# Four row tiles for a depthwise convolution: the matmul form of one stage of a two-layer kernel is replaced

## The chip, the cores and the metric

The kernel runs on one core of a Trainium2 chip, as one program. The metric is the device time of one execution in microseconds (us). The time before is the median of three runs, 3564.99 us, between 3564.83 and 3570.47.

## What is computed

Two layers run after each other on an input of 32 images, 96 channels, 56 rows and 56 columns, all in float32.

```python
# layer 0
h = conv_general_dilated(x, conv_w, (1, 1), padding=((3, 3), (3, 3)), feature_group_count=96) + conv_b
h = transpose(h, (0, 2, 3, 1))
h = (h - mean(h, -1)) * rsqrt(var(h, -1) + 1e-5) * ln_g + ln_b
h = gelu(einsum('bhwc,cf->bhwf', h, w1) + b1)
h = einsum('bhwf,fc->bhwc', h, w2) + b2
x = transpose(h, (0, 3, 1, 2)) * layer_scale + x
# layer 1
x = silu(conv_general_dilated(x, conv_w, padding 2, 5x5 taps, per channel) + conv_b)
# ... then a selective scan along the 3136 positions of every image
```

The change lies in the first convolution (7x7 taps, every channel by itself), in the layout of its output, and in the loads and stores of the MLP that follows. The second convolution and the scan have the same instructions before and after.

## The kernel before

The input comes as one array of channel, row and column, where a "row" is one of 2 x 56 (the images in two sets of 16, `j` being the set) and a row of 896 floats (`COLS`) holds 16 images of 56 columns beside each other. So the partitions hold image rows, and a vertical neighbour is another partition, a horizontal one another column.

A depthwise convolution becomes a matmul if the vertical taps are put into a matrix that multiplies rows by rows (a band matrix), one for each horizontal offset. The kernel before does this for two columns of the output at once. The input columns are separated into even and odd ones; the odd ones lie in partitions 0 to 55 of the tile `xq`, the even ones in partitions 64 to 119. The stationary matrix has 120 rows and 112 columns: 56 output rows for each of two neighbouring output columns. With 7 taps, four offsets `t` are enough, so each channel and set of images needs four matmuls with a moving operand of 448 columns (16 images x 28 column pairs), which add up in a bank of PSUM (L334). Copies of POOL (set 0), DVE (set 1) and ACT (both) bring the columns of `xt` apart into `xq` (L328, L329), so that the moving operand is contiguous within an image. A zero border of `xq` stands for the columns beyond the edge.

The band matrices are not built on the chip for each channel. A padded table `pad1` of the taps is written to memory once (`taps1_d`), and `taps_of` loads a channel's matrices by a DMA whose source addresses overlap (each row starts one step further on), into one of five tiles `wts`. In the matmul the weights of one `t` lie four floats apart (`wv`).

The loop runs over 112 jobs: the first 80 channels with both sets of images together, then the last 16 channels (`APART`) for set 0 and again for set 1, so that the statistics of set 0 are finished while set 1 is still computed. In each job ACT evicts the bank and adds the bias (L343), POOL issues two stores of the result to `conv1_d` (L347), and DVE and ACT keep the sums for the layer norm over channels: the difference to the first channel (L356), its sum (L357), its square on ACT (L358), the sum of squares (L359). `finish_norm` makes 1/standard deviation from them and writes it to `rstd_d`. Beside the loop, one entry of a list `beside` per job prepares weights of later stages. The order of instructions on an engine is made by the tile scheduler, except where `pin` keeps the program's order.

The MLP works on 28 groups of four rows. Each group has three tiles `h` of 32 channels x 4 rows, loaded from `conv1_d`; `rt`, the group's `rstd`, loaded to all channels; and three tiles of the input `x` for the residual. `normalise` multiplies h by rt on DVE (L412). `hidden` runs four row tiles of TensorE beside each other (32 rows each, one for each image row of the group, written to four banks, L422) and ACT applies gelu; `result` runs four column tiles (L441), and two DVE instructions add bias and residual and put even and odd column pairs into the output tile (L452). POOL's queue stores it to `block_d` (L464), which has four columns of a row apart from each other, as the second convolution reads them. The MLP's tiles `x`, having memory of their own, are loaded during the first convolution.

The second convolution (L535, L549, L558) uses four column tiles. The scan (L590 on) is a loop of DVE scans, products on POOL, activations and small matmuls.

Of the kernel before, what the change touches and what calls it, by code (L numbers as in the profile page):

```python
# [8 lines left out]
F32 = mybir.dt.float32  # L9
# [14 lines left out]
WP = 128  # L24
W2 = W // 2
MP = 64
P1 = (K1 + 1) // 2
# [3 lines left out]
RW = 32  # L31
QP = QW + 1
# [6 lines left out]
EPS = 1e-9  # L39
APART = 16  # L40
# [7 lines left out]
def convnext_then_scan_kernel(  # L48
# [30 lines left out]
    conv1_d = dram.tile([C, ROWS, COLS], F32, name="conv1_d")  # L79
# [3 lines left out]
    rstd_d = dram.tile([ROWS, COLS], F32, name="rstd_d")  # L83
    taps1_d = dram.tile([C, 3 * WP * P1], F32, name="taps1_d")
# [21 lines left out]

    KR = MP + H
    PQ = HALF

# [8 lines left out]

    front = ctx.enter_context(ExitStack())
    stats = front.enter_context(tc.tile_pool(name="stats", bufs=1))  # L120
    first = stats.tile([ROWS, B2, HALF], F32, name="first")
    acc1 = stats.tile([ROWS, B2, HALF], F32, name="acc1")
    acc2 = stats.tile([ROWS, B2, HALF], F32, name="acc2")
    sq = stats.tile([ROWS, B2, HALF], F32, name="sq")

    def finish_norm(j):

        a1, a2 = acc1[:, j], acc2[:, j]
        nc.vector.tensor_mul(sq[:, j], a1, a1)
        nc.vector.scalar_tensor_tensor(  # L130
            a2, in0=sq[:, j], scalar=-1.0 / C, in1=a2, op0=ALU.mult, op1=ALU.add
        )
        nc.vector.tensor_scalar(a2, a2, 1.0 / C, 0.0, ALU.mult, ALU.max)
        nc.scalar.activation(a2, a2, AF.Sqrt, bias=eps_t[:ROWS], scale=1.0)
        nc.vector.reciprocal(a1, a2)
        for s in range(2):
            nc.gpsimd.dma_start(
                rstd_d[j * H : (j + 1) * H, s * PQ : (s + 1) * PQ], a1[s * H : (s + 1) * H]
            )

    with tc.tile_pool(name="c1", bufs=3) as pool, tc.tile_pool(
        name="c1k", bufs=1
    ) as keep, tc.tile_pool(name="prep", bufs=1) as prep, tc.tile_pool(
        name="c1_ps", bufs=4, space=PSUM
    ) as psum:
        wts = [keep.tile([128, 2, H * P1], F32, name=f"wt1_{i}") for i in range(5)]
        xqs = [keep.tile([128, B2, BI, W2 + 3], F32, name=f"xq_{i}") for i in range(3)]
        jobs = [(c, (0, B2)) for c in range(C - APART)]
        jobs += [(c, (j, j + 1)) for j in range(B2) for c in range(C - APART, C)]


        kt1 = prep.tile([C, K1, K1], F32, name="kt1")
        nc.sync.dma_start(kt1, c1w.rearrange("c (i j) -> c i j", j=K1))
        xts: dict = {}

        def load_x(n):
            c, js = jobs[n]
            xts[n] = pool.tile([128, COLS], F32, name=f"xt1_{n}", tag="xt")
            for j in range(*js):
                nc.sync.dma_start(xts[n][MP * j : MP * j + H], x[c, j * H : (j + 1) * H])  # L160

# [13 lines left out]
        c1b_t = across(c1b, ROWS, C, "c1b_t", const)  # L175
        pad = prep.tile([C, 3, WP, P1], F32, name="pad1")
        nc.vector.memset(pad, 0.0)
        at = H - 1 - K1 // 2
        for i in range(3):
            for t in range(P1):  # L180
                j = 2 * t + 1 - i
                if j in range(K1):
                    nc.vector.tensor_copy(pad[:, i, at : at + K1, t], kt1[:, :, j])
        nc.sync.dma_start(taps1_d, pad.rearrange("c d p t -> c (d p t)"))
        for t in wts + xqs + [acc1, acc2]:
            nc.vector.memset(t, 0.0)
# [119 lines left out]
        def taps_of(n):  # L306

            c, wt = jobs[n][0], wts[n % len(wts)]
            for s in range(2):
                taps = bass.AP(  # L310
                    taps1_d.tensor, taps1_d.offset + (c * 3 + 1 - s) * WP * P1,
                    [[P1, H], [WP * P1, 2], [1, H * P1]],
                )
                nc.sync.dma_start(wt[MP * s : MP * s + H], taps)

        for n in range(4):
            taps_of(n)
        for n, (c, js) in enumerate(jobs):
            if n + 4 < len(jobs):
                taps_of(n + 4)  # L320
            if n + 2 < len(jobs):
                load_x(n + 2)

            xq, xt = xqs[n % len(xqs)], xts.pop(n)
            for j in range(*js):
                xv = xt[MP * j : MP * j + H].rearrange("p (i r s) -> p s i r", i=BI, s=2)
                copy = nc.vector.tensor_copy if j else nc.gpsimd.tensor_copy
                copy(xq[:H, j, :, 2 : W2 + 2], xv[:, 1])  # L328
                nc.scalar.copy(xq[MP:KR, j, :, 1 : W2 + 1], xv[:, 0])  # L329
            wv = wts[n % len(wts)].rearrange("p o m -> p (o m)").rearrange("p (q t) -> p t q", t=P1)  # L330
            ps = bank(f"ps1_{n}")[:ROWS, :, :PQ]
            for t in range(P1):
                for j in range(*js):
                    nc.tensor.matmul(  # L334
                        ps[:, j].rearrange("p (i r) -> p i r", i=BI),
                        lhsT=wv[:KR, t],
                        rhs=xq[:KR, j, :, t : t + W2],
                        start=(t == 0),
                        stop=(t == P1 - 1),
                    )  # L340
# [574 lines left out]
```

## Time and profile before

| | value |
|---|---|
| median of three runs | 3564.99 us |
| profiled execution | 3567.29 us |
| its span, first to last instruction | 3565.5 us |
| first convolution: first to last matmul of L334 | about 17.7 to 601 us |
| MLP | about 606 to 1425 us |
| second convolution | about 1425 to 1750 us |
| scan | the rest |
| PE busy over the span | 3047.3 us (85%) |
| DVE, ACT, POOL busy | 2664.8, 2351.5, 1969.4 us |
| mean granted clock of TensorE | 0.83 |

The profile is one execution on the chip. An engine's row gives its busy time; PEld is the weight load of TensorE, which runs beside matmuls. A group of instructions reads: line, engine, operation, tile written and tiles read, shapes, count, then busy time, mean nanoseconds of one instruction, and the idle time of the engine just before, with what ended it. In shapes like `32*128`, the first number is rows of the array, the second its columns. A float32 matmul leaves two records. The means of matmuls are longer than their pace, since they are pipelined: pace is busy time by count.

The input and the convolution's output are moved in these issues (the line names the tile written and the tensor read, the queue, the count and the size of one):

```
xt<-in_x_dram SPq DMA_DIRECT2D x192, 196.0 KB
x<-in_x_dram SPq DMA_DIRECT2D x336, 112.0 KB
h<-conv_d SPq DMA_DIRECT2D x336, 112.0 KB
conv_d<-ht POOLq DMA_DIRECT2D x158, 196.0 KB, 3.8
block_d<-o POOLq DMA_DIRECT2D x336, 120.0 KB, 3.1
```

### The profile page before, as it was taken

How to read it: one execution, taken by the hardware profiler on the slowest of the kernel's cores; microseconds unless marked ns; L12 is line 12 of the kernel's file. 1: busy time of each engine (PE TensorE's matmuls, PEld its weight loads, DVE VectorE, ACT ScalarE, POOL GpSimd, SP SyncE). 2: the span in 40 equal slices, each digit the busy share in tenths (PEclk: the TensorE clock that was granted, in tenths of full speed). 3: DMA queues.
4: the chain of work that ended last, by engine and by line, in shares of the span. 5: the costliest groups of instructions: out<-in, count | busy, mean ns of one | idle time of the engine just before them, and what ended most of it. 6: DMA issues, size and time to landing. Idle time of an engine off the chain costs nothing. (4 is left out here: it accounts for less than half of the span.)

```text
span 3565.5 us, 47085 instructions
## 1 busy us (share of the span) xinstructions
PE 3047.3 (85%) x17290; PEld 1291.7 (36%) x17290; DVE 2664.8 (75%) x1820; ACT 2351.5 (66%) x2168; POOL 1969.4 (55%) x1284
## 2 busy tenths in 40 slices
PE   8999999999999999799857777777777777777785
PEld 5777776333333333334322222222222222222221
DVE  6666667333333333799959999999999999999998
ACT  4555555334334333688778888888888887888885
POOL 2333343222222222000059999999899999999996
PEclk9999999999999999999956766666666666667666
DMA  6655556555555552899888787787778787887873
GB/s 185 194 178 167 173 168 197 159 159 162 162 161 164 164 159 67 244 280 290 273 257 278 264 281 261 268 279 256 264 263 270 267 272 250 290 259 260 287 255 120
DMA packets 316654, 793.97 MB, mean 223 GB/s; under 512 B 133560, under 2 KB 195024, under 8 KB 291880
## 3 DMA queue, kind: packets, MB, share of 16 engines
q1 hardware_dynamic: 269888, 671.99, 59.6%
q0 software_dynamic: 29632, 80.27, 7.0%
q10 hardware_dynamic: 16904, 38.70, 2.8%
q8 instruction: 137, 2.24, 0.3%
q14 instruction: 93, 0.76, 0.1%
HBM read 555.05 MB, written 235.74 MB: 222 GB/s over the span
## 5 line engine op out<-in xcount | busy, mean ns | idle before, releaser
L713 POOL TENSOR_TENSOR rep<-rep,bt 128x1568 f32<-128x1568 f32 x192 | 674.3, 3512 | 377.7 <-DMA rep<-du_d 377.7
L742 POOL TENSOR_TENSOR hs<-hs,ct 128x1568 f32<-128x1568 f32 x191 | 669.3, 3504 | 101.3 <-DVE hs L730 89.6
L723 DVE TENSOR_TENSOR_SCAN pv<-rep,pv 128x1568 f32<-128x1568 f32 x192 | 664.5, 3461 | 42.9 <-ACT rep L709 26.2
L432 ACT ACTIVATE g<-ph,b1p_t 128x896 f32<-128x896 f32 x336 | 320.0, 1003 | 489.7 <-PE ph L422 489.7
L452 DVE SCALAR_TENSOR_TENSOR o<-po,b2r_t,x 128x224 f32<-128x224 f32 x336 | 191.0, 611 | 545.5 <-PE po L441 534.7
L334 PE MATMUL ps<-xq,wt 120*112 120x448 f32 x1536 | 582.5, 540 | 17.7 <-DMA wt<-taps_d 17.7
L464 POOL DMA_DIRECT2D block_d<-o x336 | 183.1, 552 | 637.1 <-DVE o L452 603.9
L334 PEld LDWEIGHTS ps<-xq,wt 120*112 120x112 f32 x1536 | 429.3, 280 | 169.1 <-issue 20.2
L422 PE MATMUL ph<-h,w1r_t 32*128 32x448 f32 x4032 | 430.2, 555 | 6.9 <-DVE h L412 4.8
L641 PE MATMUL pz<-xs,wd_t 96*96 96x392 f32 x512 | 282.1, 718 | 164.6 <-ACT du L649 121.6
L441 PE MATMUL po<-g,w_t 128*32 128x448 f32 x4032 | 413.1, 543 | 0.0
L760 PE MATMUL py<-hs,sel_t 128*32 128x392 f32 x1536 | 323.1, 676 | 60.5 <-POOL hs L742 60.5
L688 PE MATMUL pk<-bn,pick_t 8*128 8x392 f32 x1024 | 291.7, 692 | 95.0 <-ACT y L769 83.1
L726 DVE SCALAR_TENSOR_TENSOR pv<-pv,rep 128x1568 f32<-128x1568 f32 x192 | 345.6, 1800 | 21.6 <-POOL rep L713 1.7
L730 DVE TENSOR_TENSOR_SCAN hs<-rep,carry_h,pv 128x1568 f32<-128x1568 f32 x96 | 334.1, 3480 | 10.0
L535 PE MATMUL ps<-xq,wt 128*32 128x448 f32 x3072 | 308.6, 549 | 37.5 <-DMA xq<-block_d 35.5
L558 DVE COPY st<-yt 28x896 f32<-28x896 f32 x288 | 318.0, 1104 | 27.8 <-ACT yt L549 17.5
L730 DVE TENSOR_TENSOR_SCAN hs<-rep,pv 128x1568 f32<-128x1568 f32 x96 | 328.4, 3421 | 9.6
L708 ACT ACTIVATE rep<-rep,lift_t 128x1568 f32<-128x1568 f32 x192 | 307.6, 1602 | 6.3
L709 ACT ACTIVATE rep<-rep,lift_t 128x1568 f32<-128x1568 f32 x192 | 307.6, 1602 | 6.3
L752 PE MATMUL py<-xs,dsm_t 96*96 96x392 f32 x512 | 300.7, 728 | 10.5 <-ACT bn L676 4.7
L707 ACT ACTIVATE rep<-rep,a_t 128x1568 f32<-128x1568 f32 x192 | 308.3, 1606 | 1.7 <-DMA rep<-du_d 1.3
(90 smaller groups left out, 3136.8 us busy)
## 6 DMA issues: line engine op xcount, KB each, us to landing
rep<-du_d SPq DMA_DIRECT2D x191, 1568.0 KB
du_d<-du SPq DMA_DIRECT2D x126, 588.0 KB
xq<-block_d SPq DMA_DIRECT2D x192, 225.0 KB
block_d<-o POOLq DMA_DIRECT2D x336, 120.0 KB, 3.1
xt<-in_x_dram SPq DMA_DIRECT2D x192, 196.0 KB
x<-in_x_dram SPq DMA_DIRECT2D x336, 112.0 KB
h<-conv_d SPq DMA_DIRECT2D x336, 112.0 KB
conv_d<-st SPq DMA_DIRECT2D x96, 392.0 KB
```

Of the source, the lines that this page charges most:

```text
L334: nc.tensor.matmul(ps[:, j].rearrange("p (i r) -> p i r", i=BI), lhsT=wv[:KR, t], rhs=xq[:KR, j, :, t : t + W2], start=(t == 0), stop=(t = ...
L422: pin(nc.tensor.matmul(phs[i // 2][:, i % 2, :HALF], lhsT=w1r_t[rows, d, f * 128 : (f + 1) * 128], rhs=hts[n, d][rows, s * HALF : (s + 1) ...
L432: nc.scalar.activation(gt, ph[:, :, :HALF], AF.Gelu, bias=b1p_t[:, f : f + 1], scale=1.0)
L441: pin(nc.tensor.matmul(po[CB * i : CB * i + CB, :HALF], lhsT=w2_t[:, f, CB * d : CB * d + CB], rhs=gts[n, s, f, i // 2][:, i % 2], start=( ...
L535: pin(nc.tensor.matmul(ps[RW * f : RW * f + RW, h, : B * QW].rearrange("p (b q) -> p b q", q=QW), lhsT=wv[:, f, t], rhs=xv[:, :, t : t + Q ...
L558: pin(copy(st[:, :, :, :, f], yt[RW * f : RW * f + QR].rearrange("p h (b q) -> p h b q", q=QW),))
L713: pin(nc.gpsimd.tensor_mul(ut, ut, bts[i // NG]))
L723: pin(nc.vector.tensor_tensor_scan(grown, da, zero, pv[:, last : last + 1] if q else 1.0 / EPS, ALU.mult, ALU.add))
L726: pin(nc.vector.scalar_tensor_tensor(run, in0=grown, scalar=1.0, in1=ut, op0=ALU.min, op1=ALU.mult))
L730: pin(nc.vector.tensor_tensor_scan(ht, da, run, carry_h[:, col : col + 1] if q else 0.0, ALU.mult, ALU.add))
L742: pin(nc.gpsimd.tensor_mul(ht, ht, cts[k]))
L760: pin(nc.tensor.matmul(py[g * DG : (g + 1) * DG, s, :BK], lhsT=sel_t, rhs=hss[k * NG + g][:, cols], start=False, stop=True, tile_position= ...
```

## The change

The first convolution is written anew. A job is now four pairs of a channel and a half `h` of the output rows: two channels with both halves (40 jobs), then for each half the last 16 channels by fours (8 jobs). Each pair takes 32 input rows (28 output rows and their neighbours inside the image) in 32 partitions, with all 32 images (1,792 columns). `load_x` brings them in as four DMAs, straight from the input, in the input's own column order; there is no `xq` and no copy into it.

`convolve` multiplies one column in four of the input (`g`, for every image and every fourth position, so the moving operand `xv[rows, g]` steps by four floats) by a matrix of 32 rows and 128 columns: 28 (of 32) output rows for each of four neighbouring output columns. Ten offsets `e` are needed for 7 taps and four columns. For six of the ten, an image's first or last column lies beyond the edge and is left out (`lo`, `hi`), so 13 of 14 positions are multiplied and written. The four pairs of the job sit in four row tiles (`tile_position=(RW * k, 0)`) and write four banks.

All ten matrices of a pair come from one tile `mat` of 13 blocks of 32 columns, seven with taps and three of zeros at each end; the matrix of `e` is the 128 columns from block `e` on. `turn` fills the seven blocks by an ACT copy from the loaded taps, which are smaller than before.

ACT evicts a job by two instructions of 896 columns or four of 448; the store is one DMA on ACT's own queue. The sums are kept for both channels of a job apart and added in `finish_norm`. The output in `conv1_d` and `rstd_d` is by half, column of four, row.

In the MLP a group is four rows of one half and two of the four columns. The loads of h and rt for the first two groups, and the first normalising, are called within the convolution's loop. The tiles `x` hold all four columns, are loaded for every second group, and come from a pool opened after the convolution's pools are closed. The result is added by one DVE instruction instead of two, and a row of four columns is stored as one piece of 7,680 bytes for each channel.

```diff
-    conv1_d = dram.tile([C, ROWS, COLS], F32, name="conv1_d")
+    conv1_d = dram.tile([C, 2, QC, RW, HALF], F32, name="conv1_d")
...
-    taps1_d = dram.tile([C, 3 * WP * P1], F32, name="taps1_d")
+    taps1_d = dram.tile([C, TP * K1], F32, name="taps1_d")
...
-        jobs = [(c, (0, B2)) for c in range(C - APART)]
-        jobs += [(c, (j, j + 1)) for j in range(B2) for c in range(C - APART, C)]
...
+        jobs = [[(c, 0), (c, 1), (c + 1, 0), (c + 1, 1)] for c in range(0, C - APART, 2)]
+        whole = len(jobs)
+        jobs += [
+            [(c + k, h) for k in range(JT)] for h in range(2) for c in range(C - APART, C, JT)
+        ]
...
+            xts[n] = pool.tile([128, 2 * COLS], F32, name=f"xt1_{n}", tag="xt")
+            for k, (c, h) in enumerate(jobs[n]):
+                nc.sync.dma_start(
+                    two(xts[n][RW * k : RW * k + RW]),
+                    x[c].rearrange("(j m) q -> m j q", m=H)[h * (H - RW) : h * (H - RW) + RW],
+                )
...
-            for j in range(*js):
-                xv = xt[MP * j : MP * j + H].rearrange("p (i r s) -> p s i r", i=BI, s=2)
-                copy = nc.vector.tensor_copy if j else nc.gpsimd.tensor_copy
-                copy(xq[:H, j, :, 2 : W2 + 2], xv[:, 1])
-                nc.scalar.copy(xq[MP:KR, j, :, 1 : W2 + 1], xv[:, 0])
-            wv = wts[n % len(wts)].rearrange("p o m -> p (o m)").rearrange("p (q t) -> p t q", t=P1)
-            ps = bank(f"ps1_{n}")[:ROWS, :, :PQ]
-            for t in range(P1):
-                for j in range(*js):
...
+            nc.scalar.copy(
+                mats[n % len(mats)][:, QC - 1 : QC - 1 + K1],
+                wts.pop(n).rearrange("p (o j) -> p j o", j=K1),
+            )
...
+            wv = mats[n % len(mats)].rearrange("p j o -> p (j o)")
+            xv = xts.pop(n).rearrange("p (b q f) -> p f b q", q=QW, f=QC)
+            pss = [bank(f"ps1_{n}_{a}") for a in range(JT // 2)]
+
+            order = sorted(range(EJ), key=lambda e: e != K1 // 2)
+            for e in order:
+
+                far, g = divmod(e - K1 // 2, QC)
+                lo, hi = max(0, -far), QW - max(0, far)
+                for k in range(JT):
+                    rows = slice(RW * k, RW * k + RW)
                     nc.tensor.matmul(
-                        ps[:, j].rearrange("p (i r) -> p i r", i=BI),
-                        lhsT=wv[:KR, t],
-                        rhs=xq[:KR, j, :, t : t + W2],
-                        start=(t == 0),
-                        stop=(t == P1 - 1),
+                        pss[k // 2][:, k % 2, :HALF].rearrange("p (b q) -> p b q", q=QW)[:, :, lo:hi],
+                        lhsT=wv[rows, RW * e : RW * e + QC * RW],
+                        rhs=xv[rows, g, :, lo + far : hi + far],
+                        start=(e == order[0]),
+                        stop=(e == order[-1]),
+                        tile_position=(RW * k, 0),
                     )
...
-            for s in range(2):
-                nc.gpsimd.dma_start(
-                    conv1_d[c, js[0] * H : js[1] * H, s * PQ : (s + 1) * PQ].rearrange(
-                        "(j m) q -> m j q", m=H
-                    ),
-                    ht[s * H : (s + 1) * H, half],
...
+            step = 2 if n < whole else 1
+            for k in range(0, JT, step):
+                c = job[k][0]
+                nc.scalar.activation(
+                    hs[:, k : k + step],
+                    pss[k // 2][:, k % 2 : k % 2 + step, :HALF],
...
+            nc.scalar.dma_start(to, hs)
...
+            def squares():
+                nc.scalar.activation(dt, dt, AF.Square)
+                for ks, _, a2 in parts:
+                    nc.vector.tensor_add(a2, a2, flat(dt[:, ks]))
...
+            pss = convolve(n)
+            if n == whole + len(jobs[whole:]) // 2:
+                finish_norm(0)
+            hs = evict(n, pss)
...
+            squares = add_sums(n, hs)
+            if n + 1 < len(jobs):
+                squares()
+            if n >= 2 and beside:
                 beside.pop(0)()
-            if n == C + 1:
-                finish_norm(0)
...
+            if n == len(jobs) - 3:
+                load_rows(0)
+                load_rows(1)
+            if n == len(jobs) - 2:
+                for d in range(blocks):
+                    normalise(0, d)
...
-            for e in range(2):
-                pin(nc.vector.scalar_tensor_tensor(
-                    ot[:, 2 * e + s, :, e : e + QW],
-                    in0=po[:, :HALF].rearrange("p (i a e) -> p e i a", i=BI, e=2)[:, e],
...
+            pin(nc.vector.scalar_tensor_tensor(
+                ot[:, f].rearrange("p (b r) -> p b r", r=QP)[:, :, at : at + QW],
+                in0=po[:, :HALF].rearrange("p (b q) -> p b q", q=QW),
+                scalar=b2r_t[:, d : d + 1],
+                in1=xts[n // 2, d].rearrange("p (b q f) -> p f b q", q=QW, f=QC)[:, f],
```

## The prediction, made before the changed kernel was run

> **What bounds the kernel now.** I read four views in this order. First the page: its slices of the span, and the groups of the line that is replaced.
>
> ```profile
> span 3565.5 us, 47085 instructions
> PE   8999999999999999799857777777777777777785
> ...
> L334 PE MATMUL ps<-xq,wt 120*112 120x448 f32 x1536 | 582.5, 540 | 17.7 <-DMA wt<-taps_d 17.7
> ...
> L334 PEld LDWEIGHTS ps<-xq,wt 120*112 120x112 f32 x1536 | 429.3, 280 | 169.1 <-issue 20.2
> L422 PE MATMUL ph<-h,w1r_t 32*128 32x448 f32 x4032 | 430.2, 555 | 6.9 <-DVE h L412 4.8
> ```
>
> Second the busy times by stage, with stretches cut at the first and last matmul of L334 (columns: length, then PE, PEld, DVE, ACT, POOL busy, clock, DMA share, GB/s).
>
> ```profile
> 17.70:601.00 583.30, 583.29 (x1546) 430.55 (x1546) 367.07 (x470) 307.57 (x413) 192.71 (x317) 1.00 0.61 183
> 601.00:612.00 11.00, 5.49 (x30) 2.47 (x28) 10.15 (x13) 3.67 (x6) 5.84 (x9) 0.84 0.75 232
> 612.00:1425.00 813.00, 811.61 (x8000) 302.79 (x8004) 269.67 (x413) 319.94 (x336) 178.41 (x327) 1.00 0.50 149
> ```
>
> The reader is to see that PE works without a gap for 583.3 us of convolution and for 811.6 of 813.0 us of MLP, at full clock, while DVE is at 63% and DMA at 61% in the first. TensorE bounds both, so what the first convolution costs TensorE is what it costs the kernel. The second convolution and the scan, from about 1425 us on, have the same instructions on both sides and keep their time.
>
> Third the timeline of one channel in the middle of the first convolution. L343 evicts at 300.09 and again at 306.12: 6.03 us a channel, which is 16 passes of 377 ns (a float32 matmul leaves two records; I call each a pass).
>
> ```profile
> 300.09 1.01 ACT L343 ACTIVATE ht<-ps,c1b_t 112x896 f32<-112x896 f32 x1 [0.16 <-PE ps L334]
> ...
> 302.25 1.09 DVE L357 TENSOR_TENSOR acc<-acc,dt 112x896 f32<-112x896 f32 x1
> 303.44 0.95 ACT L358 ACTIVATE dt<-dt 112x896 f32<-112x896 f32 x1 [1.72 <-DVE acc L357]
> 304.42 1.09 DVE L359 TENSOR_TENSOR acc<-acc,dt 112x896 f32<-112x896 f32 x1 [1.08 <-ACT dt L358]
> ...
> 306.12 1.01 ACT L343 ACTIVATE ht<-ps,c1b_t 112x896 f32<-112x896 f32 x1 [0.15 <-PE ps L334]
> ```
>
> Last the groups by shape, for what an access costs that steps over elements: the weight loads,
>
> ```profile
> L535 PEld LDWEIGHTS ps<-xq,wt 128*32 128x32 f32 x3072 | 133.2, 141 | 213.0 <-issue 194.6 <-ACT st L558 12.1 <-DMA xq<-block_d 4.1
> L441 PEld LDWEIGHTS po<-g,w_t 128*32 128x32 f32 x4032 | 114.1, 109 | 274.2 <-issue 223.4 <-DVE h L412 50.8
> ...
> L250 PEld LDWEIGHTS ps_b<-lnb_t,w_t 96*128 96x128 f32 x6 | 0.8, 190 | 0.3 <-issue 0.2
> L247 PEld LDWEIGHTS ps_w<-w1g,cen 96*96 96x96 f32 x2 | 0.3, 162 | 0.3 <-issue 0.2
> ```
>
> and, in the second convolution, a copy of ACT that writes one float in four:
>
> ```profile
> L558 ACT COPY st<-yt 28x896 f32<-28x896 f32 x96 | 195.8, 2040 | 53.9 <-DMA conv_d<-st 52.7
> ```
>
> These rows carry the forecast. With contiguous columns 96 take 162 ns and 128 take 190: 0.875 ns a column over a fixed 78. L334's weights lie four floats (16 bytes) apart: (280 - 78)/112 = 1.80 ns a column. L535's lie eight floats apart: 32 columns cost 32 ns more than L441's contiguous 32, so 1.88. TensorE reads float32 weights at half speed once each lies 16 bytes or more from the last. ACT shows the same: from the squares (448 elements 576 ns, 896 elements 950) it has 202 ns fixed and 0.835 an element, but writing every fourth float in L558 takes (2040 - 202)/896 = 2.05.
>
> **What the Trainium skill says.** "SBUF — State Buffer", section "Door 1: The DMA port swizzle", describes 16-byte lines that give full bandwidth only when hit at least twice; the loads above agree. The same note puts the free step at four float32 elements; L334's 1.80 against 0.875 contradicts that, and the measurement decides. "TensorE: Matmul & The Clock Gate", section "LDWEIGHTS", prices a load by its columns alone, P/1.2 ns; the slope of 0.875 agrees for contiguous weights, not for stepped ones. The same page, Part 3, gives 3.07 times for four row tiles side by side. Here L422, in the very form that the change uses, needs 430.2/4032 = 107 ns a pass against 379 for L334: 3.6 times. No page says how fast a stepped moving operand streams, and no matmul of this trace has one.
>
> **The change part by part.**
>
> *Matmuls of the first convolution.* Removed: 768 matmuls, two passes of 448 columns, 688,128 column steps in 582.5 us, 0.8465 ns a step. Added: 48 jobs of ten input columns; for each, four row tiles beside each other, so the set of four costs the steps of one. Four of the ten sets are 448 columns wide, six are 416: 2 x (4 x 448 + 6 x 416) = 8,576 steps a job, 411,648 in all. Contiguous, that would be 348.5 us. But the moving operand is read from x as it lies, every fourth float, where before xq was contiguous. Contiguous float32 weights go in at 0.875 ns an element and contiguous moving data at 0.8465, the same pace, so I expect the same halving. Bounds: 0.8465 ns a step if the moving path hides it (348.5 us), 2.05, as in ACT's stepped copy (844 us). I take twice 0.8465, 1.693: 697 us, 14.5 a job, **114.5 more than before**. The six narrower sets also write PSUM in runs of 13, which no row of the trace shows; I give that nothing, and the range's upper side holds it. The weights are now contiguous and load under the matmuls.
>
> *Beside it, per job of 14.5 us.* DVE: three operations on 1,792 elements. From 624 ns for 448 and 1,092 for 896 (1.045 an element, 156 fixed) each is 2.03, so 6.1 us. ACT: two evictions of 1.01, the square 202 + 1792 x 0.835 = 1.70, and the new turn of the taps, 128x224, 0.4 contiguous and 0.7 at half speed, so 4.4 us. DVE's order is strict: difference, first sum, then the second sum, which waits for ACT's square; the next difference is queued behind it. ACT in turn has the next eviction behind that square. The ring costs 2.03 + 2.03 + 0.1 + 1.70 + 0.05 + two evictions 2.02 = 7.95 us: free under 14.5, dear if the matmuls are fast. Gone are the xq copies of ACT, DVE and POOL, none on the path.
>
> *DMA.* A job moves 917 KB in, 917 KB out, 115 KB of taps: 1.95 MB per 14.5 us, 134 GB/s, below the 183 of now. Stores move from POOL's queue to ACT's; issuing is short beside ACT's 10 us of slack.
>
> *Start.* PE waits 17.7 us for taps. The table is smaller (183 KB for 590), but eight loads of x of 229 KB stand before it on SP's queue where four of 196 did, and a turn follows: -2 to +3, taken as +1.
>
> *Passage to the MLP.* Today PE idles about 6.9 us there, 4.8 of it for DVE's normalised h. The first half's norm is now finished at job 44, with three jobs behind it, and the first h are normalised in the loop: -5 (0 to -7). The loads of x for the MLP can no longer come early, as their memory is the convolution's: 2.75 MB, some 11 us at the 250 GB/s that the scan's slices of the page reach, while PE has 12 us of hidden layer before the first result asks for them and two result banks after that. Nothing, up to +8 if that cover fails.
>
> *MLP and its end.* The same passes in the same order, so 812 us. DVE's two additions of 611 ns become one of 448 elements, 0.6 to 1.1 us, with DVE idle two thirds of the time: nothing. Stores of block_d become whole rows, but the last are twice as large, 240 KB, with the second convolution waiting for them: +3 (0 to +6).
>
> *Sum* on the profiled execution: 3567.3 + 114.5 + 1 - 5 + 3 = 3680.8; the median of the runs shown is 2.3 lower. With 1.70 instead of 1.693 ns (the loads suggested 1.80 to 1.88) another 3 us: **3682 us**.
>
> **The rivals.**
>
> *Full-speed moving operand (ends faster).* Mechanism: the moving path streams steps of 16 bytes at 0.8465 ns. For it: nothing in the trace shows a stepped moving operand, and it is a read port of its own. Against: weights, and ACT's writes, all halve. Matmuls then take 7.26 us a job, the ring of DVE and ACT 7.95 takes over: 40 x 7.95 + 8 x 8.5 (four short evictions, sums in halves) = 386, plus some 8 us of backlog before the MLP: 3567.3 - 582.5 + 386 + 8 - 2.3 = 3376 us. It decides below 582.5/411,648 = 1.415 ns a step; above that the kernel is slower.
>
> *Partly slowed*, 1.0 to 1.6 ns a step: 412 to 659 us, so 3395 to 3642; half of it on either side.
>
> *Tiles one after another.* The change then doesn't do what it says: 4 x 348.5 = 1394 us, 4377. Against it L422's 107 ns in the same form, with the same four banks.
>
> **How the numbers follow.** Half speed or slower 0.83, full speed 0.11, partly 0.04, serial 0.02. The range runs from 3645 (half speed less the edges, and the upper end of partly) to 3800 (1.98 ns a step); left out are full speed, most of partly, serial, and 0.05 of the forecast's own case. Only cases of one sign hold most of the chance. A measurement here tells about 0.2% (7 us) from no change. Faster: 0.11 + 0.02 = 0.13; within: 0.01; slower: 0.86.
>
> **What would show it.** Right: sets of four matmuls of L368 every 0.70 to 0.76 us, PE without gaps, jobs 14.5 us apart, DVE and ACT each below half busy, DMA share below 0.5. Wrong: sets every 0.36 us and idle PE before L368 released by ACT's evictions, which is the first rival; or matmuls of one set following each other, which is the last. The MLP should stay at about 812 us of PE. A gap of over 5 us after the last L368, released by the DMA of x, would break the passage.

## The result: 4.4% slower, and the profile after

| | before | after |
|---|---|---|
| median (range, runs) | 3565.36 us (3564.83 to 3570.47, 4) | 3723.52 us (3721.39 to 3724.39, 4) |
| ratio, 95% interval | | 1.0439 [1.0421, 1.0457] |
| span of the profiled execution | 3565.5 us | 3721.6 us |
| first convolution, first matmul to last | 17.7 to 601 | 24.1 to 759.2 |

The forecast was 3682 us in a range of 3645 to 3800; the time is 41.5 us above the forecast and inside the range. These are lines of the page of the changed kernel: the span, TensorE's row of slices, and the groups of the new matmul and its weight loads.

```profile
span 3721.6 us, 49078 instructions
...
PE   7999999999999999989976777787777787777775
...
L368 PE MATMUL ps<-xt,mat 32*128 32x416 f32 (+1 forms) x3840 | 733.8, 936 | 24.1 <-ACT mat L351 24.1
...
L368 PEld LDWEIGHTS ps<-xt,mat 32*128 32x128 f32 x3840 | 445.8, 204 | 308.2 <-issue 256.8
```

TensorE was busy for 582.5 us in the first convolution before; now it is busy for 733.8, and its only idle time is the 24.1 us at the start. The busy times by stage (length, PE, PEld, DVE, ACT, POOL, clock, DMA share, GB/s) say what holds it:

```profile
24.10:759.20 735.10, 735.09 (x3850) 446.94 (x3850) 303.51 (x178) 202.03 (x206) 0.73 (x1) 1.00 0.45 133
759.20:784.00 24.80, 16.89 (x102) 7.45 (x104) 15.42 (x13) 14.03 (x15) 8.79 (x6) 0.72 0.87 206
784.00:1580.00 796.00, 796.00 (x7864) 296.42 (x7860) 245.41 (x243) 312.21 (x328) 75.39 (x156) 1.00 0.50 150
```

In the convolution PE has no gap, at full clock; DVE is at 41%, ACT at 27%, DMA at 45%. Nothing but the matmul itself can be the limit. The timeline of one job shows its pace. The weight loads stand for the matmuls here, four loads to a set: one pass of 448 or 416 columns, done by four row tiles at once. The first two load lines belong to sets of 416 columns, the last two to sets of 448.

```profile
300.69 1.01 ACT L388 ACTIVATE hs<-ps,c1b_t 128x896 f32<-128x896 f32 x1 [7.21 <-PE ps L368]
...
303.97 0.52 PEld L368 LDWEIGHTS ps<-xt,mat 32*128 32x128 f32 x4 [0.23 <-issue]
304.71 0.52 PEld L368 LDWEIGHTS ps<-xt,mat 32*128 32x128 f32 x4 [0.23 <-issue]
...
308.48 0.61 PEld L368 LDWEIGHTS ps<-xt,mat 32*128 32x128 f32 x4 [0.18 <-issue]
309.27 0.60 PEld L368 LDWEIGHTS ps<-xt,mat 32*128 32x128 f32 x4 [0.18 <-issue]
...
315.94 1.01 ACT L388 ACTIVATE hs<-ps,c1b_t 128x896 f32<-128x896 f32 x1 [7.21 <-PE ps L368]
```

From load to load over several sets, a set of 416 columns takes 0.745 us, one of 448 takes 0.787, and a job has 12 of the first and 8 of the second: 15.24 us. The evictions at 300.69 and 315.94 are one job apart, 15.25 us. The tiles do run side by side: one after another, a set would take four passes of 377 ns. The eviction waits 7.21 us for the matmuls, so ACT follows and doesn't lead.

Where the 156 us of span come from (each from the views shown here, before against after):

| part | us |
|---|---|
| matmuls of the first convolution, 733.8 against 582.5 | +151.3 |
| first matmul at 24.11, not 17.71 | +6.4 |
| last matmul of the convolution to last matmul of the MLP, 830.9 against 827.3 | +3.6 |
| PE's gap ahead of the second convolution, 11.32 against 13.62 | -2.3 |
| the rest, second convolution and scan | -2.9 |

The +6.4 is in the timeline of the start:

```profile
1.20 12.83 SPq L190 DMA_DIRECT2D xt<-in_x_dram  x8
...
15.25 0.33 SPq L212 DMA_DIRECT2D taps_d<-pad  x1
...
19.73 5.42 SPq L343 DMA_DIRECT2D wt<-taps_d  x12
```

The table of taps is in its tile `pad` by 4.5 us, but its store is issued only at 15.25, behind eight issues of x that took SP's queue 12.83 us; then the round trip through memory and ACT's turn follow. At the passage to the MLP the three idle times of PE are:

```profile
760.48 4.97 PE L504 MATMUL ph<-h,w1r_t 32*128 32x448 f32 x28 [1.26 <-ACT hs L388]
768.84 4.04 PE L504 MATMUL ph<-h,w1r_t 32*128 32x448 f32 x24 [3.39 <-ACT g L514]
776.14 7.76 PE L504 MATMUL ph<-h,w1r_t 32*128 32x448 f32 x44 [3.26 <-ACT g L514]
```

Before, there were two:

```profile
606.30 4.97 PE L422 MATMUL ph<-h,w1r_t 32*128 32x448 f32 x28 [4.78 <-DVE h L412]
613.02 2.25 PE L422 MATMUL ph<-h,w1r_t 32*128 32x448 f32 x12 [1.75 <-ACT g L432]
```

The wait for DVE's first h is gone, as forecast, but in place of one wait of 1.75 us for ACT's gelu there are two, of 3.39 and 3.26. ACT takes the square root of the second half's norm between two gelus there: it loads its tables three times (1.28 us each; two of the three are shown) and waits 2.1 us for DVE's variance (L133).

```profile
769.70 1.28 ACT L134 ACT_TABLE_LOAD   x1
773.10 0.67 ACT L134 ACTIVATE acc<-acc,eps_t 128x448 f32<-128x448 f32 x1 [2.11 <-DVE acc L133]
773.78 1.28 ACT L514 ACT_TABLE_LOAD   x1
```

The page's group of the hidden layer sums it up (before: 430.2 us busy, 6.9 idle):

```profile
L504 PE MATMUL ph<-h,w1r_t 32*128 32x448 f32 x4032 | 432.9, 558 | 7.9 <-ACT g L514 6.6
```

So 1.0 of the 3.6 us is idle time. The rest is busy time, and it falls in the stretch of these waits (759.20 to 784.00 above, with a mean granted clock of 0.72): after it the mean of a hidden-layer matmul is 551 ns on both sides.

### The profile page after: what moved, and what is told of

Its sections match the earlier page's. It is cut to its first block, busy times and chain, and to the rows that moved or that the text cites. A ratio compares the mean times of both kernels' runs of the same rounds, so it can differ in the third digit from the quotient of the medians.

```text
span 3721.6 us, 49078 instructions
## 1 busy us (share of the span) xinstructions
PE 3195.8 (86%) x19594; PEld 1305.0 (35%) x19594; DVE 2581.1 (69%) x1370; ACT 2249.4 (60%) x1963; POOL 1676.2 (45%) x796
## 5 line engine op out<-in xcount | busy, mean ns | idle before, releaser
L368 PE MATMUL ps<-xt,mat 32*128 32x416 f32 (+1 forms) x3840 | 733.8, 936 | 24.1 <-ACT mat L351 24.1
L536 DVE SCALAR_TENSOR_TENSOR o<-po,b2r_t,x 128x448 f32<-128x448 f32 x168 | 170.5, 1015 | 564.8 <-PE po L523 552.3
L368 PEld LDWEIGHTS ps<-xt,mat 32*128 32x128 f32 x3840 | 445.8, 204 | 308.2 <-issue 256.8
L547 POOL DMA_DIRECT2D block_d<-o x168 | 81.2, 490 | 734.9 <-DVE o L536 678.8
```

What stands on the lines that cost most here:

```text
L368: nc.tensor.matmul(pss[k // 2][:, k % 2, :HALF].rearrange("p (b q) -> p b q", q=QW)[:, :, lo:hi], lhsT=wv[rows, RW * e : RW * e + QC * RW] ...
```

## The experiments

The theory, from the prediction: the step of four floats in the moving operand is the whole loss, and with contiguous data the ring of DVE and ACT becomes the bound. Rivals: the narrower sets, a fixed cost for each set, or the four tiles hindering each other. Each edit is against the changed kernel unless another is named. Ratios are to the kernel before on the same chip, with the 95% interval; a single run has none.

**The step taken out, and halved, and made three.** The same matmuls read the tile with another view, and so multiply other columns.

```diff
-            xv = xts.pop(n).rearrange("p (b q f) -> p f b q", q=QW, f=QC)
+            xv = xts.pop(n).rearrange("p (f b q) -> p f b q", q=QW, f=QC)
```

For a step of two floats, and of three (which reads the first three quarters of the tile), the view and its index are:

```diff
+            xv = xts.pop(n).rearrange("p (t b q f) -> p t f b q", t=2, q=QW, f=2)
...
+                        rhs=xv[rows, g // 2, g % 2, :, lo + far : hi + far],
```

```diff
+            xv = xts.pop(n)[:, : 3 * HALF].rearrange("p (b q f) -> p f b q", q=QW, f=3)
...
+                        rhs=xv[rows, g % 3, :, lo + far : hi + far],
```

> The only edit is the view of the moving operand in the changed kernel's matmul: 448 (or 13 of each 14) neighbouring floats instead of every fourth, so the columns multiplied are other ones than the convolution's; sizes, weights, tiles, PSUM writes and all other work stay. Theory (a step of 16 bytes halves the stream of the moving operand, and nothing else is slow): L368 falls from 733.8 us to about 348 us of work, a set of four from 0.75-0.79 us to about 0.36; then the ring of DVE and ACT (difference, sum, square, second sum, evictions) sets a job at about 8.0 us, so the stage takes some 386 us and the kernel about 3723 - 734 + 386 + 8 = 3383 us, under 3400. Rival (the tile form itself is slow: runs of 13 written to PSUM, four banks, 128 weight columns loaded for each set): the pace stays at 0.75 us a set and the time within 1% of 3723. Rival (partly the step, partly the form): between 3450 and 3650.

> The moving operand steps by two floats (8 bytes) instead of four; again other columns than the convolution's, all else as in the changed kernel. Theory A (full pace as long as each 16-byte line is hit twice): as with contiguous columns, about 0.36 us a set and about 3383 us. Theory B (every step beyond one element costs): a set at 0.5 us or more, L368 over 480 us, the kernel over 3460.

> The moving operand steps by three floats (12 bytes), so that of four elements three open a new line; other columns than the convolution's. Theory A1 (each new 16-byte line costs two cycles[...], a second hit in it is free):[...] a set of 448 at about 0.56 to 0.6 us, L368 some 520 to 550 us, the kernel about 3510 to 3540. Theory A2 (a threshold at a step of 16 bytes, full pace below): about 0.36 us a set and 3383 us. Theory A3 (half pace as soon as a line is not hit twice by neighbours): 0.75 us and 3723.

Measured: 3391.32 us for the contiguous view (ratio 0.9507 [0.9491, 0.9523]), 3396.26 for two floats and 3549.43 for three (a single run each). The contiguous view alone takes 332 us off the changed kernel and makes it faster than the one before. The sets, from the timelines of a job as above (for one float from the kernel with the pinned order below, where no set waits), beside the number of 16-byte lines that a set's read goes through. A run of an image is 14 positions in the wide sets and 13 in the narrow, and lines are counted from the view, each run of neighbouring reads in one line once:

| step | set of 448, us | lines | set of 416, us | lines |
|---|---|---|---|---|
| 1 float | 0.374 | 112 | 0.351 | 112 |
| 2 floats | 0.394 | 224 | 0.395 | 224 |
| 3 floats | 0.59 | 336 | 0.567 | 320 |
| 4 floats (the change) | 0.787 | 448 | 0.745 | 416 |

The lines behind the table. For one float, two loads before sets of 448:

```profile
308.02 0.20 PEld L368 LDWEIGHTS ps<-xt,mat 32*128 32x128 f32 x4 [0.17 <-issue]
308.40 0.20 PEld L368 LDWEIGHTS ps<-xt,mat 32*128 32x128 f32 x4 [0.17 <-issue]
```

For two floats, sets of 448 and then of 416:

```profile
308.07 0.21 PEld L368 LDWEIGHTS ps<-xt,mat 32*128 32x128 f32 x4 [0.18 <-issue]
308.46 0.21 PEld L368 LDWEIGHTS ps<-xt,mat 32*128 32x128 f32 x4 [0.18 <-issue]
...
310.43 0.22 PEld L368 LDWEIGHTS ps<-xt,mat 32*128 32x128 f32 x4 [0.17 <-issue]
310.83 0.22 PEld L368 LDWEIGHTS ps<-xt,mat 32*128 32x128 f32 x4 [0.17 <-issue]
```

For three floats, the sets of 416 and then of 448:

```profile
308.20 0.23 PEld L368 LDWEIGHTS ps<-xt,mat 32*128 32x128 f32 x4 [0.33 <-issue]
308.77 0.23 PEld L368 LDWEIGHTS ps<-xt,mat 32*128 32x128 f32 x4 [0.33 <-issue]
...
311.12 0.21 PEld L368 LDWEIGHTS ps<-xt,mat 32*128 32x128 f32 x4 [0.38 <-issue]
311.71 0.21 PEld L368 LDWEIGHTS ps<-xt,mat 32*128 32x128 f32 x4 [0.38 <-issue]
```

The widest step gives 0.787/448 = 1.757 ns a line. With that price the other stepped sets come out at 224 x 1.757 = 0.394 (measured 0.394 and 0.395), 336 x 1.757 = 0.590 (0.59) and 320 x 1.757 = 0.562 (0.567); 112 lines would be 0.197, and there the floor of 0.835 ns a column stands (448 x 0.835 = 0.374). So in these runs a pass pays the larger of two sums: 0.835 ns for each column, or 1.757 ns for each new line. That it is lines and not bytes is seen at two floats: 13 positions touch seven lines as 14 do, and the narrow set is no shorter than the wide one. Only the narrow set of the change itself is clearly off, 0.745 for 416 x 1.757 = 0.731.

Two of the rivals go with the first row. The four tiles don't hinder each other: side by side they take 0.374 us, where one pass of as many columns took 0.377 alone in the kernel before (120 rows, contiguous). And the narrower sets, which write PSUM in runs of 13, take 0.351 for 416 x 0.835 = 0.347.

The Trainium skill's "SBUF — State Buffer", section "Door 1: The DMA port swizzle", speaks of 16-byte lines that need two hits for full bandwidth. The runs nearly agree: at two floats, so two hits, a column costs 0.88 ns for 0.835. Its "4 fp32" as the free stride is contradicted, as by the weight loads before: at four floats a column costs 1.757 ns.

The contiguous view also shows the next bound. The timeline of one job of it:

```profile
308.30 2.02 DVE L433 TENSOR_TENSOR acc<-acc,dt 128x1792 f32<-128x1792 f32 x1 [1.76 <-ACT dt L431]
...
310.25 2.02 DVE L416 TENSOR_TENSOR dt<-hs,first 128x1792 f32<-128x1792 f32 x1
312.30 2.02 DVE L428 TENSOR_TENSOR acc<-acc,dt 128x1792 f32<-128x1792 f32 x1
314.36 1.70 ACT L431 ACTIVATE dt<-dt 128x1792 f32<-128x1792 f32 x1 [3.80 <-DVE acc L428]
315.96 1.89 ACT L388 ACTIVATE hs<-ps,c1b_t 128x896 f32<-128x896 f32 x2
316.08 2.02 DVE L433 TENSOR_TENSOR acc<-acc,dt 128x1792 f32<-128x1792 f32 x1 [1.76 <-ACT dt L431]
```

DVE's second sum (L433) waits for the square, ACT's evictions come after the square, and DVE's next difference after both: 7.78 us from one L433 to the next, the ring that the prediction put at 7.95. The matmuls need 8 x 0.374 + 12 x 0.351 = 7.2 and wait. The step of two floats lies just beside it: 20 sets of 0.395 make 7.9 us a job, so its time is near the contiguous view's.

**More and shorter sets** (eight of the ten sets cut in two halves of the images).

```diff
-                for k in range(JT):
+                cuts = [(0, B)] if e in (order[0], order[-1]) else [(0, BI), (BI, B)]
+                for (s, z), k in [(cut, k) for cut in cuts for k in range(JT)]:
```

> The changed kernel, stepping by 16 bytes, with eight of the ten column sets of a job cut into two matmuls of half the width (16 images each): the same column steps, 36 sets of four a job instead of 20. It is to place the 37 to 48 us by which L368's 733.8 us exceeds exact half pace. Theory F (a fixed cost of about 0.04 to 0.05 us for each set): 768 more sets cost 31 to 38 us, L368 some 765 to 772 us, the kernel about 3755 to 3762. Theory P (a share of each step, 1.78 instead of 1.69 ns): L368 stays at 734 +- 6 us, the kernel at 3723.

Measured: 3726.70 us (a single run). With 36 sets a job for 20, the matmuls are busy for 735.8 us where they were for 733.8:

```profile
L369 PE MATMUL ps<-xt,mat 32*128 32x208 f32 (+3 forms) x6912 | 735.8, 599 | 23.0 <-DMA wt<-taps_d 23.0
```

That is 2 us for 768 more sets, under 0.003 us a set, so a fixed cost of 0.04 us or more for each set is out. What makes the narrow sets of the change 0.014 us longer than their lines wasn't separated.

**The columns brought apart by POOL** (a tile `xq`, filled by a copy one job ahead).

```diff
+            nc.gpsimd.tensor_copy(
+                xq.rearrange("p (f t) -> p f t", f=QC),
+                xts.pop(n).rearrange("p (t f) -> p f t", f=QC),
+            )
...
-            xv = xts.pop(n).rearrange("p (b q f) -> p f b q", q=QW, f=QC)
+            xv = xqs.pop(n).rearrange("p (f b q) -> p f b q", q=QW, f=QC)
```

> The convolution as it is meant, with the input's columns brought apart by POOL: one copy of 128x1792 a job from the loaded tile into a tile where each of the four column sets is contiguous, one job ahead. POOL has nothing else to do there. Theory (the step is the whole loss): the matmuls run at 0.36 us a set; POOL's copy, read in steps of 16 bytes, takes 2 to 5 us of a job of 8.0, so the ring of DVE and ACT is the bound and the time about 3385 us, 5% faster than the kernel before. Rival (POOL's stepped copy is slower than 8 us, or slows DVE through shared access): POOL sets the job, 9 to 15 us, 3430 to 3700 us. Rival (the form is slow): 3723 or above.

Measured: 3498.11 us, ratio 0.9809 [0.9794, 0.9824]. The gain is there, 1.9% against the kernel before, but it is 107 us less than with the contiguous view. From its timeline:

```profile
299.26 3.67 POOL L361 COPY xq<-xt 128x1792 f32<-128x1792 f32 x1 [9.29 <-PE ps L379]
...
299.56 5.25 DVE L427 TENSOR_TENSOR dt<-hs,first 128x1792 f32<-128x1792 f32 x1
304.85 2.02 DVE L439 TENSOR_TENSOR acc<-acc,dt 128x1792 f32<-128x1792 f32 x1
...
307.03 3.42 POOL L361 COPY xq<-xt 128x1792 f32<-128x1792 f32 x1 [4.11 <-DMA xt<-in_x_dram]
...
308.63 3.71 DVE L444 TENSOR_TENSOR acc<-acc,dt 128x1792 f32<-128x1792 f32 x1 [1.76 <-ACT dt L442]
```

DVE's difference, 2.03 us otherwise, takes 5.25: it ends 1.9 us after POOL's copy does, as if it had started only then. In the next job the copy meets the second sum (L444), which takes 3.71 for 2.02 and again ends 1.9 us after the copy. The ring of DVE and ACT holds these times whole: jobs take 11.0 and 9.5 us in turn, 7.78 plus 3.22 and plus 1.69. The Trainium skill's "SBUF — State Buffer", section "🔬 SBUF: two separate sides", says this: a DVE operation with two inputs in SBUF and a GpSimd operation that reads SBUF share a pair of ports; the one that starts first holds it for the whole instruction, and the other is blocked. The trace agrees.

**The input laid out by column of four**, so that no copy and no step is needed: the array's order changes, and the residual's view follows.

```diff
-        "x": v["x"].reshape(B2, BI, C, H, W).transpose(2, 0, 3, 1, 4).reshape(C, ROWS, COLS),
+        "x": v["x"].reshape(B2, BI, C, H, QW, QC).transpose(2, 0, 3, 5, 1, 4).reshape(C, ROWS, COLS),
...
-            xv = xts.pop(n).rearrange("p (b q f) -> p f b q", q=QW, f=QC)
+            xv = xts.pop(n).rearrange("p (j f b q) -> p f j b q", j=B2, q=QW, f=QC)
```

> The changed kernel on an input that is laid out by column of four in each row of 896 (four runs of 16 images x 14 columns, instead of 16 images x 56), in the array that the program is given; views in the convolution and in the MLP's residual follow, nothing else changes. Every moving operand of the first convolution is then contiguous, and so is the residual's read. Theory (the step is the loss, wherever it is taken away): the same time as with the contiguous view that multiplied other columns, 3391 +- 8 us, and DVE's residual addition falls from 1.02 to about 0.62 us without moving the time. Rival (something of the data or of a fourth dimension in the operand's address matters): over 3410.

Measured: 3389.17 us, 0.9505 [0.949, 0.9521]: the contiguous view's time, with the whole computation in it. The residual of the MLP, which also reads x, falls from 1,015 to 684 ns without effect on the end, as it is off the path.

**The ring opened, first try:** on the laid-out input, and on the input as it lies with the copy shared by ACT (two of the four column sets) and DVE (the other two), the square's sum of a job is called one job later (and the tile `dt` has three buffers for two).

```diff
+            if owed:
+                owed.pop()()
             if n + 1 < len(jobs):
-                squares()
+                owed.append(squares)
```

> As the kernel with the input laid out by column of four, and the second sum of a job (with ACT's square) is taken after the next job's difference and first sum. This opens the ring of DVE and ACT, which was 7.78 us a job. Theory (the ring is what holds the contiguous form): jobs fall to TensorE's own 7.1 to 7.3 us, so 48 x 0.55 = 26 us less: about 3365. Rival (DMA holds it: its share was already 0.88 at 7.78 us a job, 255 GB/s): jobs stay at 7.6 us or more, waits of L368 or of ACT's copies go to DMA, 3380 to 3391 us.

> The convolution on the input as it lies, with the second sums taken late, and the columns brought apart half by ACT (two of the four sets) and half by DVE, one job ahead, instead of by POOL. DVE: 6.1 us of sums and about 1.1 to 2.0 us for its half; ACT: 4.2 us and about 1.8 us. Theory: neither engine reaches TensorE's 7.3 us by much, jobs of 7.3 to 8.1 us, 3365 to 3405 us in all, so 4.5 to 5.5% faster than before without touching the input's layout, and DVE's sums stay at 2.03 us, as POOL no longer shares with it. Rival (the copies lengthen each other's waits into a new ring): over 3420.

Measured: 3396.40 us (0.9526 [0.9511, 0.954]) and 3436.51 (0.964 [0.9626, 0.9655]). The first says nothing of the ring: the scheduler put the sums back to their old place, and DVE waits the same 1.76 us for the square. The second has the copies in the unopened ring: 8.7 us a job. The split copy still beats the kernel before.

**The ring opened, second try:** the same two kernels with the evictions, differences, squares and sums in `pin`, so that the program's order holds.

```diff
-                nc.scalar.activation(dt, dt, AF.Square)
+                pin(nc.scalar.activation(dt, dt, AF.Square))
                 for ks, _, a2 in parts:
-                    nc.vector.tensor_add(a2, a2, flat(dt[:, ks]))
+                    pin(nc.vector.tensor_add(a2, a2, flat(dt[:, ks])))
```

> The kernel with the input laid out by column of four and the second sums taken late, as before, but now with differences, sums, squares and evictions held in the program's order: in the last run the scheduler had put each second sum back behind its own square (the same 1.76 us wait on every job), so that run did not test the ring. Theory (the ring holds the contiguous form): DVE 6.2 us and ACT 4.6 us a job lie under TensorE's 8 x 0.374 + 12 x 0.355 = 7.25 us, the wait of 1.76 us is gone, jobs of 7.25 to 7.35 us and 3389 - 40 x 0.5 - 8 x 1.1 = about 3360 us. Rival (DMA holds it, 0.88 busy at 7.78 us): jobs of 7.6 us and more, 3378 to 3391 us, L368 waiting for xt or for taps.

> The convolution on the input as it lies, columns brought apart half by ACT and half by DVE, second sums late, now in the program's order. In the last run the ring stood with DVE's copy inside it: 8.7 us a job. Theory: DVE 6.1 + 1.0 + 0.1 = 7.2 us, ACT 1.9 + 0.6 + 1.7 + 1.9 + 0.4 = 6.5 us, TensorE 7.25: jobs of 7.3 to 7.5 us and 3362 to 3380 us, 5.2 to 5.8% faster than before. Rival (DMA or a new ring through the three buffers of xq): 8 us a job and more, over 3395.

Measured: 3367.35 us (0.9443 [0.9427, 0.9458]) and 3374.42 (0.9462 [0.9448, 0.9477]). The ring is gone: a job takes 7.2 us, the matmuls' own time. For the split copy, the stage by busy time:

```profile
100.00:390.00 290.00, 289.10 (x3202) 174.44 (x3198) 274.96 (x172) 226.37 (x206) 0.73 (x1) 1.00 0.91 260
```

PE is the bound again, with DVE at 95% beside it, ACT at 78% and the DMA engines at 91%: little is left to gain in this stage. But a new wait has come at its end, of about 15 us in both (PE, and then ACT, of the split copy):

```profile
406.96 6.13 PE L521 MATMUL ph<-h,w1r_t 32*128 32x448 f32 x28 [15.09 <-DVE h L170]
```

```profile
379.44 2.19 ACT L399 ACTIVATE hs<-ps,c1b_t 128x448 f32<-128x448 f32 x4
395.02 0.37 ACTq L411 DMA_DIRECT2D conv_d<-hs  x1
395.44 1.70 ACT L442 ACTIVATE dt<-dt 128x1792 f32<-128x1792 f32 x1 [13.80 <-DMA h<-conv_d]
```

DVE's first h is named, but ACT stands still before it. A store of the convolution's output (L411) is at the head of its queue until 395.02, when the MLP's first loads of h from that tensor are done. With jobs of 15.25 us this wait had room; with 7.2 it has not.

**The last stores on another queue** (against the split copy, pinned).

```diff
-            nc.scalar.dma_start(to, hs)
+            (nc.scalar if n < whole + 4 else nc.gpsimd).dma_start(to, hs)
```

> The split-copy kernel with pinned late sums, with one thing changed: the stores of the last four jobs are issued from GpSimd's queue instead of ACT's. In the kernel without this change ACT stands still for 13.8 us before the MLP (idle ended by the DMA of h), with a store at the head of its queue, and PE then waits 15.09 us for DVE's normalised h. Theory Q (a store on ACT's own queue waits for the loads of h, and evictions, squares and sums are queued behind it): the evictions of the last two jobs and the first h come some 11 to 13 us earlier, PE's gap before the MLP falls from 15.1 to below 5 us, time 3362 to 3366 from 3374.4. Theory R (the first h is late because the norm's values come late from memory, whatever ACT does): the gap stays at 13 to 16 us and the time at 3372 to 3377.

Measured: 3365.01 us (3358.56 to 3367.93), 0.9436 [0.942, 0.9452]. The store now waits in POOL's queue, where nothing that matters is behind it, and the last squares and evictions come on time:

```profile
386.16 1.70 ACT L442 ACTIVATE dt<-dt 128x1792 f32<-128x1792 f32 x1 [0.45 <-DVE acc L439]
...
392.64 0.75 POOL L411 DMA_DIRECT2D conv_d<-hs  x1 [5.89 <-DMA h<-conv_d]
...
395.77 5.49 PE L521 MATMUL ph<-h,w1r_t 32*128 32x448 f32 x28 [5.06 <-DVE h L170]
```

PE's gap falls from 15.09 to 5.06 us, a hair more than theory Q allowed, and the MLP starts 11.2 us earlier. The ratio's interval still overlaps that of the kernel without this edit (0.9448 to 0.9477), so the gain is read from the two traces. This is the best version on the input as it lies: 5.6% faster than the kernel before, where the change was 4.4% slower.

**The start** (the taps' store and the first three jobs' taps moved to POOL's queue).

```diff
-        nc.sync.dma_start(taps1_d, pad.rearrange("c p j -> c (p j)"))
+        nc.gpsimd.dma_start(taps1_d, pad.rearrange("c p j -> c (p j)"))
...
-                nc.sync.dma_start(
+                (nc.sync if n > 2 else nc.gpsimd).dma_start(
```

> The changed kernel with the store of the tap table and the taps of the first three jobs on POOL's queue instead of SP's, where they stood behind eight and more loads of x. Theory (the late start, 24.1 us against 17.7, is the wait on SP's queue): the first matmul at 11 to 15 us, 9 to 13 us less, about 3712 us. Rival (the transfers themselves are late, behind 1.8 MB of x in the DMA engines, whichever queue issues them): first matmul at 20 us or later, 3719 or more.

Measured: 3723.73 us (two runs). The store is issued at 4.03 and the first matmul comes at 18.40, 5.7 us earlier but later than expected: ACT's turn now stands behind another instruction, which waits for a DMA.

```profile
16.37 1.28 ACT L312 ACT_TABLE_LOAD   x1 [16.37 <-DMA xt<-in_x_dram]
17.66 0.20 ACT L312 ACTIVATE a_t<-a_t 128x3 f32<-128x3 f32 x1
17.77 1.07 ACT L351 COPY mat<-wt 128x224 f32<-128x224 f32 x2
18.40 1.94 PE L368 MATMUL ps<-xt,mat 32*128 32x448 f32 x8 [18.40 <-ACT mat L351]
```

The 5.7 us last to the second convolution, which starts at 1594.89 for 1601.41, but not to the end: its span is 1.6 us shorter. From that start to the end the fourteen profiles of this case, with the same instructions there, took 2120.2 to 2129.4 us; the changed kernel's is the shortest of them, and this one's 2125.1. So the SP queue did cost the start 5.7 us, and whether the time would gain from it is below what two runs can tell.

## Why the prediction was right

*The bound.* Right. PE alone holds the first convolution on both sides, and the stepped moving operand is what made it dearer: taken out, it returns 332 us, and the time falls below that of the kernel before. The argument by likeness, from stepped weight loads to a stepped moving operand, held.

*The size of the matmul term.* Too small by 37 us of 114.5. The step "I take twice 0.8465, 1.693" was mis-sized: measured are 1.757 ns a column in the wide sets and 1.79 in the narrow, 1.783 in the mean over 411,648. The stepped weight loads, 1.80 and 1.88 ns in the kernel before, were the nearer guide: what sets the pace is not half the rate of the matmul but the price of a line, 1.757 ns, and 1.757/0.835 is 2.1. Of the 37 us, 26 come from 1.757 instead of 1.693 (0.064 x 411,648), and 8 from the narrower sets (1.79 for 1.757 ns on 48 x 12 x 416 columns), to which the prediction gave nothing; 3 are left over. Jobs 15.25 us apart for 14.5 is the same error. The prediction's premise that four row tiles cost the steps of one held: 0.374 us for 0.377.

*Beside it, and DMA.* Right: DVE, ACT and DMA all below half, at 133 GB/s, and the evictions wait for PE. The ring was right too, though hidden here: 7.78 us for 7.95 when the contiguous view uncovered it. (The addends given there make 7.93, and those of the whole forecast 3681.4 for 3682; neither matters.)

*Start.* Forecast +1 with +3 as its edge, measured +6.4. The prediction saw the eight loads ahead of the taps, but not what they cost: SP's queue was occupied for 12.83 us by their issue.

*Passage to the MLP.* Forecast -5. DVE's wait did go, but the MLP as a whole begins no earlier: the gelus wait for ACT, which the second half's norm occupies at that point, and the stretch to the last matmul of the MLP is 3.6 us longer. The question "what is late next" was put for the loads of x alone, which were in time, and not for ACT.

*MLP and its end.* Its pace held after the passage. The +3 for larger last stores didn't come; PE's gap before the second convolution is 2.3 us shorter. The smaller terms missed by +5.4 us (start), +8.6 (passage), -5.3 (end) and -2.9 (what follows, within the spread of the profiles): that they add up to only about 6 is luck. The direction and the range rest on the matmul term.

*The rivals.* The full-speed case was put at 3376 us. The kernel with the contiguous view is that case made real, and took 3391: its start is 5.6 us later than before for the forecast's 1, its convolution takes 389 us for 386, and PE's gap before the MLP is 15.06 for the 8 allowed. Tiles one after another were excluded by the pace of the first job.

## What to carry to other kernels

A matmul's moving operand was cheap to step only while two elements shared 16 bytes: count the lines that it goes through. In this form (float32, row tiles of 32) a step of two is nearly free, three cost 1.6 times and four 2.1 times. Where the price of an access couldn't be seen, the same access on another path of the same engine, here the weight load, was the best guide, and its own number was better than a round factor. Before a copy that makes an operand contiguous is taken out as overhead, count its elements beside other work against the matmul's columns on the path; and when a stage is then sped up, look for the ring behind it and for stores at the head of a compute engine's queue.

## What the hardware showed that was not expected

- The price of a stepped moving operand is a price per new 16-byte line, 1.757 ns, against a floor of 0.835 ns a column: 448 columns take 0.374, 0.394, 0.59 and 0.787 us at steps of one to four floats.
- POOL's copy of 1,792 elements held DVE's operation with two inputs off until the copy had ended: 5.25 us for 2.03, and 3.71 for 2.02 where the copy had started earlier.
- Four row tiles side by side took no longer than one pass alone: 0.374 us for 448 contiguous columns, against 0.377 in the kernel before.
- Reading every fourth float, ACT's copy of 896 elements took 1,849 ns, and DVE's of as many 992 (the split copy, pinned). With the fixed parts used in the prediction (202 and 156 ns) that is an estimate of 1.84 ns an element on ACT, about 2.2 times its contiguous 0.835, and of 0.93 on DVE. The kernel before has the same kind of copy reading every second float, 448 elements at a time: 607 ns on ACT (L329), so 0.90 an element and nearly free, and a median of 390 ns on DVE (L328), so 0.52. From a step of two to one of four DVE paid too, 1.8 times; no run has this copy contiguous.
- The stage from the second convolution on, with the same instructions, differs by up to 9 us between profiles, more than most of the small terms of a forecast like this one.
